# One attention and gating kernel: layer 1's lanes of two samples kept apart, and the output product moved to the head of its place

## Chip, core and metric

The kernel runs on one core of one Trainium2 chip. The metric is the device time of one execution in microseconds (us). Before the change it took 3711.0 us (median of the 3 executions known before the change was run, 3706.7 to 3712.3). Every run told of below was in the fast state, except one that was timed only once and has no state; it is named. Outputs of all kernels were correct.

## The reference, cut to what matters

Four layers are applied to x, four samples of 256 channels of 48 x 48. Each adds its result to x, and each reads x through a group norm.

```python
x = x + L0(gn(x))   # eight-head attention over 2304 places, q and k normalised, then w_out
x = x + L1(gn(x))   # max pool, blur, 81-tap depthwise sums, sigmoid gate, x * gate
x = x + L2(gn(x))   # a second attention, one head
x = x + L3(gn(x))   # depthwise 3 x 3 and norms
```

What matters here: layer 0 is nearly all matmuls; layer 1 has none (for the first three samples), so it can run beside the *next* sample's layer 0 on the other engines. Both write x.

## The kernel before

Layer 0 is cut into groups. A group issues the scores of two key blocks and weighs the values of the two blocks before. Nine groups are a unit (384 queries of two heads), six units a phase (one sample, one pair of heads). Each engine executes its instructions in the order in which the program records them, and the recorder below decides that order.

```python
for t, (u, g, st) in enumerate(groups):
    for j in range(g * G, (g + 1) * G):
        scores(u, j)                     # TensorE, then exp on ScalarE
    if prev is not None:
        add_up(*prev)                    # sums of exps: VectorE, some on GpSimd
    do(due, t)
    ...
    if clock["slot"] == AT_AFTER % NG:   # third group: an early layer-1 step
        lanes([lane for lane in st["others"] if lane[1] == FREE], st, t, ends)
    do(fills, t)                         # the place's products
    lanes(st["others"], st, t + 0.5, ends)   # layer-1 steps
    ... weigh(pu, j) ...
```

The third group of a unit is "the place": it also holds a projection chunk for the next pair of heads and the output product of an earlier unit, sorted by rank.

```python
# chunk: q, then v, then k, squares and the next fetch
return [(1, lambda: qk(s, 0)), (2, lambda: values(s)), (3, end)]

def part(k):                 # one half of the output product
    ps = pj_tile()           # one of two PSUM buffers, in turn
    nc.tensor.matmul(ps[:, :SL], lhsT=wo[...], rhs=o["o"], start=True, stop=True)
    nc.vector.scalar_tensor_tensor(xs, ps[:, :SL], pair["bo"][...], xs, ALU.add, ALU.add)

return [((2.5, 4)[k], lambda k=k: part(k)) for k in range(NK)]
```

Layer 1 of a sample is a generator (a "lane") that takes one step in some groups. Its long middle part is rounds of four products on ScalarE and one sum on VectorE. Rounds may stand in groups with the indices 2, 5, 8 of a unit, for sample 2 in 2, 4, 6, 8; all other steps in `(2, 2, 3, 5, 6, 8)`. With three rounds a unit, a lane does not end within its sample's four phases, and its tail runs beside the next lane.

```python
TURNS, ROUND, HASTE = (2, 2, 3, 5, 6, 8), -1, -2
ROUND_TURNS = {ROUND: (2, 5, 8), HASTE: (2, 4, 6, 8)}
...
if b > 0:
    end = n - 2 if (b, p) == (B - 1, NPAIR - 1) else n + 1
    others.append((l1[b - 1], FREE, 2 if p == 0 else 0, end))
if b > 1 and p == 0:
    others.append((l1[b - 2], FREE, 0, 4 * NG))     # the tail of the lane before
```

Of the kernel before, what the change touches and what calls it, by code (L numbers as in the profile page):

```python
# [17 lines left out]
NK = 2  # L18
# [56 lines left out]
def usual_path(  # L75
# [156 lines left out]
    def scores(u, j):  # L232
        ps = sc_tile()
        for c in range(2):
            for h in range(2):
                r = slice(h * D, (h + 1) * D)
                j0 = j * P + c * D
                nc.tensor.matmul(  # L238
                    ps[c * D : (c + 1) * D, h, :SL], lhsT=u["of"]["k"][r, j0 : j0 + D],
                    rhs=u["of"]["q"][r, u["qc"]],  # L240
                    start=True, stop=True,
                )
        pt = ppool.tile([P, 2, SL], F32, tag="pt", name="pt")
        nc.scalar.activation(pt, ps[:, :, :SL], AF.Exp, scale=u["scale"])  # L244
        u["pt"][j] = pt
# [139 lines left out]
    def attend(phases):  # L385


        groups = []
        for units, work, others in phases:
            for slot, fns in work.items():  # L390
                fills.setdefault(len(groups) + slot, []).extend(fns)
            st = {"others": [[gen, n, a, z, 0, 0] for gen, n, a, z in others], "at": 0}
            groups += [(u, g, st) for u in units for g in range(NG)]
        prev = None

        def lanes(some, st, t, ends):
            for lane in some:
                gen, n, a, z, done, ready = lane
                until = -(-n * (st["at"] + 1 - a) // (z - a))
                clock["final"] = final = st["at"] == z - 1  # L400
                while final or (done < until and t >= ready and not ends):
                    wait = next(gen, None)
                    if wait is None:
                        break
                    done, ready = done + 1, t + wait
                lane[4:] = done, ready

        def do(table, t):

            jobs = [job if isinstance(job, tuple) else (5, job) for job in table.pop(t, ())]  # L410
            for _, fn in sorted(jobs, key=lambda job: job[0]):
                fn()

        for t, (u, g, st) in enumerate(groups):
            for j in range(g * G, (g + 1) * G):
                scores(u, j)
            if prev is not None:
                add_up(*prev)
            do(due, t)

            ends = prev is not None and prev[1] == NG - 1
            clock["t"], clock["slot"] = t, st["at"] % NG

            clock["early"] = True
            if clock["slot"] == AT_AFTER % NG:
                lanes([lane for lane in st["others"] if lane[1] == FREE], st, t, ends)
            do(fills, t)
            clock["early"] = False
            lanes(st["others"], st, t + 0.5, ends)
            st["at"] += 1  # L430
            if prev is not None:
                pu, pg = prev
                for j in range(pg * G, (pg + 1) * G):
                    weigh(pu, j)
                if pg == NG - 1:
                    last(pu, t)
            prev = (u, g)
        pu, pg = prev
        add_up(pu, pg)
        for j in range(pg * G, (pg + 1) * G):  # L440
            weigh(pu, j)
        last(pu, len(groups))
        for t in sorted(set(due) | set(fills)):
            do(fills, t)
            do(due, t)
# [132 lines left out]
    def out_proj(b, p, c, pair, o):  # L578

        cols = slice(c * SL, (c + 1) * SL)  # L580

        def part(k):
            ps = pj_tile()
            nc.tensor.matmul(  # L584
                ps[:, :SL], lhsT=wo[:, p, k * P : (k + 1) * P], rhs=o["o"], start=True,
                stop=True,
            )
            xs = X[b][:, k, cols]
            nc.vector.scalar_tensor_tensor(  # L589
                xs, ps[:, :SL], pair["bo"][:, k : k + 1], xs, ALU.add, ALU.add  # L590
            )

        return [((2.5, 4)[k], lambda k=k: part(k)) for k in range(NK)]

    def l0_unit(b, p, c, pair):
        hold = {}
# [68 lines left out]
    ]  # L665
    L1_BUF = (NT + 1) * AS * AS

    TURNS, ROUND, HASTE = (2, 2, 3, 5, 6, 8), -1, -2
    ROUND_TURNS = {ROUND: (2, 5, 8), HASTE: (2, 4, 6, 8)}

    def paced(gen):

        at, count, wait, turns = -9, 0, 0, TURNS
        while True:
            t, slot = clock["t"], clock["slot"]
            count = count if t == at else 0
            most = turns.count(slot)
            if clock["early"]:
                most = 1 if turns == TURNS else 0
            if not clock["final"] and (t < at + wait or count >= most):  # L680
                yield 0.5
                continue
            wait = next(gen, None)
            if wait is None:
                return
            at, count = t, count + 1
            turns = ROUND_TURNS.get(wait, TURNS)
            yield 0

    def maxima(b, k, res):  # L690
# [60 lines left out]

    def strips(b, k, norm, res):


        haste = HASTE if b == NX - 1 else ROUND
        pd = padded(k, norm, res)

        bufs = [
            lp.tile([P, L1_BUF], F32, tag=tag, name="prod").rearrange("p (n s) -> p n s", s=NT + 1)
            for tag in ("t1", "t2", "t3")  # L760
        ]

        def products(n):
            for i, t in enumerate(ROUNDS[n]):
                dr, dc = TAPS[t]
                nc.scalar.activation(  # L766
                    bufs[n % 3][:, :, min(n, 1) + i].rearrange("p (r c) -> p r c", c=AS),
                    pd[:, PAD + dr : PAD + dr + AS, PAD + dc : PAD + dc + AS],
                    AF.Identity, scale=wt[:, k, t : t + 1],
                )  # L770

        products(0)
        yield haste
        products(1)
        yield haste
        for n, taps in enumerate(ROUNDS):
            last = n == len(ROUNDS) - 1
            if n + 2 < len(ROUNDS):
                products(n + 2)
            to = bufs[(n + 1) % 3][:, :, 0]  # L780
            if last:
                res["acc"] = lp.tile([P, AS, AS], F32, tag="l1acc", name="l1acc")
                to = res["acc"].rearrange("p r c -> p (r c)")
            nc.vector.tensor_reduce(  # L784
                to, bufs[n % 3][:, :, : min(n, 1) + len(taps)], AX.X, ALU.add
            )
            yield haste

    TAPS_AT_ONCE = 12

# [370 lines left out]
    for i, (b, p) in enumerate(order):  # L1161
        work, others = {}, []
        if i + 1 < len(order):
            new = projs[i + 1]
            work[0] = [new["start"]]
            for s in range(NCH):
                work[NG * s + AT_CHUNK] = new["chunk"](s)
            work[NG + AT_CHUNK].append(new["out_bias"])
            for slot, fn in zip((n - 5, n - 3, n - 2, n - 1), new["scale"]):
                work[slot] = [fn]  # L1170
            if i + 2 < len(order):
                work[n // 2] = [projs[i + 2]["prefetch"]]
                work[NG * (NCH - 1) + AT_CHUNK].append(projs[i + 2]["norms"])
        else:
            start, slices = project2(0, norms2[0], twos[0])
            work[1] = [start]
            for s in range(NSL):
                work[NG * s + AT_CHUNK] = slices[s]
        if (b, p) == (2, 0):
            for s in range(NSL):  # L1180
                work.setdefault(s + 2 * NG, []).append(lambda s=s: send(s))
                work.setdefault(s + 5 * NG, []).append(lambda s=s: receive(s))
        if (b, p) == (0, 0):
            others.append((tap_weights(), WEIGHT_TICKS, 2, n - 2))
        if b > 0:
            end = n - 2 if (b, p) == (B - 1, NPAIR - 1) else n + 1
            others.append((l1[b - 1], FREE, 2 if p == 0 else 0, end))
        if b > 1 and p == 0:
            others.append((l1[b - 2], FREE, 0, 4 * NG))
        if (b, p) == (B - 1, NPAIR - 1):  # L1190
            others.append((part(ahead, L1_AHEAD, False), L1_AHEAD, n - L1_AHEAD - 3, n))
        if p == 1 and b + 1 < B:
            others.append((gn(b + 1, norms0[b + 1]), GN_TICKS, 0, n - 2))
        phases.append(([l0_unit(b, p, c, pairs[b][p]) for c in range(NCH)], work, others))
# [1261 lines left out]
```

## Time and profile before

The prediction below shows the profile's lines; this table has what the argument uses. "Wait in places" is worked out from the starts of the score matmuls in the trace: the length of each third group less the length of a free one, that is, of one of the same kind in which TensorE waits for no other engine's late work. A phase with two lanes is called a double phase.

| | before |
|---|---|
| span of the profiled execution | 3710.8 us |
| TensorE busy | 95% |
| phase without layer 1 | 179.0 us |
| phase with one lane | 180 to 184.5 us |
| phases with two lanes | 197.7 and 195.7 us |
| ordinary group, free place | 2.58 us, 8.34 us |
| wait in places, all layer 0 | 40.6 us, 28.2 of it in the two double phases |

TensorE has no slack in layer 0. So each microsecond that it waits in a place is a microsecond of the span, and work that stays on the other engines costs nothing unless TensorE waits for it.

### The profile page before, as it was taken

The numbers are of one execution on the slowest core, as the hardware profiler recorded it, in microseconds if no ns is written. First come the engines' busy times: TensorE is split into PE (matmuls) and PEld (weight loads), VectorE is DVE, ScalarE is ACT, GpSimd is POOL, SyncE is SP. The second block draws the span as 40 slices with busy tenths as digits, with TensorE's granted clock in tenths as the row PEclk, the third lists the DMA queues.
The fourth block names the chain that finished last, engine by engine and source line by source line (L and its number), as shares of the span: only waits on it lengthen the run. The fifth ranks groups of instructions, "written<-read, shape, count | busy, mean of one in ns | idle before, by whom it ended". The sixth has DMA issues, their size and how long they took to land.

```text
span 3710.8 us, 86538 instructions
## 1 busy us (share of the span) xinstructions
PE 3522.4 (95%) x36330; PEld 1759.4 (47%) x36330; DVE 2588.3 (70%) x3203; ACT 2344.5 (63%) x3819; POOL 1444.7 (39%) x900
## 2 busy tenths in 40 slices
PE   7999999999999999999999999999999998999685
PEld 4444444454444444444444444444444445654343
DVE  2455555476778777967787779767968786576687
ACT  4665666666776677557766775587578555555353
POOL 2333333333334333433343334433433455664242
PEclk9999999999999999999999999999999999999797
DMA  4111111111111111121111111111111100000001
GB/s 138 24 25 21 26 21 26 21 25 21 25 21 26 20 29 17 34 55 34 21 25 21 25 21 25 21 25 21 25 16 25 17 6 6 6 8 4 26 29 74
DMA packets 114591, 97.89 MB, mean 26 GB/s; under 512 B 56224, under 2 KB 111632, under 8 KB 112400
## 3 DMA queue, kind: packets, MB, share of 16 engines
q1 hardware_dynamic: 111728, 91.27, 12.8%
q8 instruction: 286, 4.69, 0.5%
q10 hardware_dynamic: 2464, 1.00, 0.1%
q14 instruction: 113, 0.93, 0.1%
HBM read 59.33 MB, written 11.80 MB: 19 GB/s over the span
## 4 chain that ended last, share of the span: by engine, by line
PE 68%; DVE 18%; issue 5%; ACT 4%; POOL 3%; DMA 2%; SPq 0%; DVEq 0%; ACTq 0%; POOLq 0%
PE av L258 26%; PE sc L238 26%; DVE acc L284 7%; PE pj L512 6%; PE pj L584 3%; PE pj L533 3%; DVE sc L1446 2%; PE pj L291 1%; POOL half L269 1%; ACT pt L244 1%; DVE av L1446 1%; DVE acc L278 1%; PE pj L828 1%; ACT prod L766 1%; DMA xs<-in_x_dram 1%
## 5 line engine op out<-in xcount | busy, mean ns | idle before, releaser
L244 ACT ACTIVATE pt<-sc 128x768 f32<-128x768 f32 x1944 | 1476.5, 812 | 814.1 <-PE sc L238 805.4
L269 POOL TENSOR_TENSOR half<-pt 128x768 f32<-128x768 f32 x477 | 954.1, 2001 | 1673.4 <-ACT pt L244 1611.7
L238 PE MATMUL sc<-q,k 64*64 64x384 f32 x13824 | 1279.6, 485 | 12.7 <-ACT pt L244 9.9
L258 PE MATMUL av<-pt,v 64*64 64x384 f32 x13824 | 1279.8, 485 | 0.0
L284 DVE TENSOR_TENSOR acc<-acc,pt 128x768 f32<-128x768 f32 x792 | 930.7, 1175 | 86.2 <-DVE acc L284 1.8
L238 PEld LDWEIGHTS sc<-q,k 64*64 64x64 f32 x13824 | 510.6, 133 | 638.2 <-issue 499.9
L258 PEld LDWEIGHTS av<-pt,v 64*64 64x64 f32 x13824 | 514.4, 133 | 594.0 <-issue 557.3
L284 DVE TENSOR_TENSOR acc<-acc,half 128x768 f32<-128x768 f32 x459 | 468.6, 1021 | 335.7 <-POOL half L269 334.1
L589 DVE SCALAR_TENSOR_TENSOR x<-pj,bo,x 128x384 f32<-128x384 f32 x192 | 118.0, 615 | 461.9 <-PE pj L584 461.7
L512 PE MATMUL pj<-xs,w 128*128 128x384 f32 (+1 forms) x768 | 298.5, 512 | 3.2 <-issue 1.7
L766 ACT ACTIVATE prod<-pd,wt 128x256 f32<-128x256 f32 x486 | 280.6, 743 | 0.2
L339 POOL TENSOR_TENSOR o<-o,rinv 128x384 f32<-128x384 f32 x95 | 128.9, 1356 | 284.3 <-DMA rinv<-rinv 273.2
L512 PEld LDWEIGHTS pj<-xs,w 128*128 128x128 f32 x768 | 131.0, 190 | 157.3 <-issue 53.9
L584 PE MATMUL pj<-o,wo 128*128 128x384 f32 x384 | 159.8, 501 | 33.3 <-DVE x L589 28.7
L258 PE MATMUL av<-pt,qv 64*64 64x384 f32 x1728 | 173.9, 496 | 0.0
L238 PE MATMUL sc<-qv,kd 64*64 64x384 f32 x1728 | 169.4, 486 | 2.4 <-ACT pt L244 2.4
L784 DVE TENSOR_REDUCE prod<-prod 128x256 f32<-128x1280 f32 x114 | 168.5, 1478 | 0.0
L278 DVE TENSOR_TENSOR acc<-pt 128x768 f32<-128x768 f32 x99 | 139.3, 1407 | 26.4 <-ACT pt L244 26.4
L533 PEld LDWEIGHTS pj<-w,xs 128*128 128x128 f32 x1152 | 143.8, 192 | 26.0 <-issue 0.6
L533 PE MATMUL pj<-w,xs 128*128 128x128 f32 x1152 | 144.1, 275 | 0.0
L518 ACT ACTIVATE k<-pj,bias 128x384 f32<-128x384 f32 x96 | 55.7, 580 | 127.5 <-PE pj L512 127.0
L335 POOL TENSOR_TENSOR o<-raw 128x384 f32<-128x384 f32 x95 | 117.7, 1238 | 0.0
(226 smaller groups left out, 2686.7 us busy)
## 6 DMA issues: line engine op xcount, KB each, us to landing
xs<-in_x_dram SPq DMA_DIRECT2D x96, 384.0 KB
rinv<-rinv SPq DMA_DIRECT2D x208, 94.5 KB
x<-in_x_dram SPq DMA_DIRECT2D x6, 1152.0 KB
out_dram<-x SPq DMA_DIRECT2D x6, 1152.0 KB
l<-row SPq DMA_DIRECT2D x416, 1.5 KB
w<-in_wqkv_dram SPq DMA_DIRECT2D x32, 192.0 KB
rinv<-ls SPq DMA_DIRECT2D x208, 1.5 KB
x_out<-x SPq DMA_DIRECT2D x6, 384.0 KB
```

Source lines behind the costliest of these rows:

```text
L238: nc.tensor.matmul(ps[c * D : (c + 1) * D, h, :SL], lhsT=u["of"]["k"][r, j0 : j0 + D], rhs=u["of"]["q"][r, u["qc"]], start=True, stop=True,)
L244: nc.scalar.activation(pt, ps[:, :, :SL], AF.Exp, scale=u["scale"])
L258: nc.tensor.matmul(u["av"][h * D : (h + 1) * D, half, :SL], lhsT=value(u, j, h)[r], rhs=pt[r, h, :], start=j == 0, stop=j == JB - 1,)
L269: nc.gpsimd.tensor_add(half, pts[0], pts[1])
L278: nc.vector.tensor_add(u["acc"], ready[0], ready[1])
L284: nc.vector.tensor_add(u["acc"], u["acc"], term)
L339: eng.tensor_mul(o, o, u["rinv"])
L512: nc.tensor.matmul(ps[:, :n], lhsT=at["w"][:, k, t, :], rhs=xs[s][:, k, :n], start=k == 0, stop=k == NK - 1,)
L533: nc.tensor.matmul(ps[:, i * P : (i + 1) * P], lhsT=xs[s][:, k, i * P : (i + 1) * P], rhs=at["w"][:, k, 2, :], start=k == 0, stop=k == NK - 1,
L584: nc.tensor.matmul(ps[:, :SL], lhsT=wo[:, p, k * P : (k + 1) * P], rhs=o["o"], start=True, stop=True,)
L766: nc.scalar.activation(bufs[n % 3][:, :, min(n, 1) + i].rearrange("p (r c) -> p r c", c=AS), pd[:, PAD + dr : PAD + dr + AS, PAD + dc : PA ...
L784: nc.vector.tensor_reduce(to, bufs[n % 3][:, :, : min(n, 1) + len(taps)], AX.X, ALU.add)
```

## The change

It has two intents. The lanes of two samples shall never run at once: rounds stand in four of nine groups for every sample, and a lane must end in its own last phase. And the output product shall come first in the place, with its addition to x recorded ahead of the group's sums and of the early layer-1 step, so that nothing stands before it.

```diff
-        def do(table, t):
+        def do(table, t, which=lambda rank: True):
 (the jobs that `which` takes are done, the others stay)
         for t, (u, g, st) in enumerate(groups):
             for j in range(g * G, (g + 1) * G):
                 scores(u, j)
+            do(fills, t, lambda rank: rank < 1)
             if prev is not None:
                 add_up(*prev)
-        return [((2.5, 4)[k], lambda k=k: part(k)) for k in range(NK)]
+        return [((0, 4)[k], lambda k=k: part(k)) for k in range(NK)]
-    TURNS, ROUND, HASTE = (2, 2, 3, 5, 6, 8), -1, -2
-    ROUND_TURNS = {ROUND: (2, 5, 8), HASTE: (2, 4, 6, 8)}
+    TURNS, ROUND, ROUND_TURNS = (2, 2, 3, 5, 6, 8), -1, (2, 4, 6, 8)
-                work.setdefault(s + 2 * NG, []).append(lambda s=s: send(s))
-                work.setdefault(s + 5 * NG, []).append(lambda s=s: receive(s))
+                work.setdefault(s, []).append(lambda s=s: send(s))
+                work.setdefault(s + NG, []).append(lambda s=s: receive(s))
-            end = n - 2 if (b, p) == (B - 1, NPAIR - 1) else n + 1
+            end = n - 2 if p == NPAIR - 1 else n + 1
-        if b > 1 and p == 0:
-            others.append((l1[b - 2], FREE, 0, 4 * NG))
```

(Cut: the renaming of `haste` in the rounds, and the body of `do`.)

More of the change, by code (lines that the diff above doesn't have):

```diff
@@ L406, in lanes @@
                 lane[4:] = done, ready
-        def do(table, t):
+        def do(table, t, which=lambda rank: True):
             jobs = [job if isinstance(job, tuple) else (5, job) for job in table.pop(t, ())]
-            for _, fn in sorted(jobs, key=lambda job: job[0]):
+            table[t] = [job for job in jobs if not which(job[0])]
+            for _, fn in sorted((job for job in jobs if which(job[0])), key=lambda job: job[0]):
                 fn()
@@ L686, in paced @@
             at, count = t, count + 1
-            turns = ROUND_TURNS.get(wait, TURNS)
+            turns = ROUND_TURNS if wait == ROUND else TURNS
             yield 0
@@ L752, in strips @@
     def strips(b, k, norm, res):
-        haste = HASTE if b == NX - 1 else ROUND
         pd = padded(k, norm, res)
@@ L772, in strips @@
         products(0)
-        yield haste
+        yield ROUND
         products(1)
-        yield haste
+        yield ROUND
         for n, taps in enumerate(ROUNDS):
@@ L786, in strips @@
             )
-            yield haste
+            yield ROUND
     TAPS_AT_ONCE = 12
```

## The prediction

> **What bounds the kernel now.** I read the page's busy shares and its chain first, then busy time in windows that I cut at the attention's own borders, then the list of waits, then the timeline of single places.
>
> ```profile
> PE 3522.4 (95%) x36330; PEld 1759.4 (47%) x36330; DVE 2588.3 (70%) x3203; ACT 2344.5 (63%) x3819; POOL 1444.7 (39%) x900
> ...
> PE 68%; DVE 18%; issue 5%; ACT 4%; POOL 3%; DMA 2%; SPq 0%; DVEq 0%; ACTq 0%; POOLq 0%
> ```
>
> TensorE is busy 95% of the span and holds 68% of the chain; VectorE has 18% of the chain though it is busy only 70%: it matters in places, not on average. Layer 0 is 16 phases (sample, head pair) of 54 groups, nine groups to a unit. A group (scores and weighing of two key blocks) takes 2.58 us, and the third group of each unit, "the place", takes 8.34 us, as it also holds a projection chunk and the output product of an earlier unit. Cut at phase borders (from the starts of every 16th score matmul):
>
> ```profile
> 586.60:765.60 179.00, 178.95 (x1932) 89.07 (x1928) 91.16 (x124) 108.41 (x172) 58.51 (x38) 1.00 0.14 24
> 765.60:948.70 183.10, 180.78 (x1936) 88.73 (x1932) 132.03 (x173) 115.54 (x187) 70.79 (x40) 1.00 0.13 21
> 948.70:1131.70 183.00, 182.72 (x1936) 86.78 (x1932) 141.15 (x161) 141.48 (x240) 66.30 (x39) 1.00 0.14 23
> ...
> 1498.10:1695.80 197.70, 185.46 (x1944) 89.48 (x1940) 153.54 (x200) 116.13 (x188) 77.59 (x44) 0.97 0.20 44
> ...
> 2245.60:2441.30 195.70, 184.01 (x1944) 89.03 (x1940) 154.78 (x203) 118.22 (x192) 77.29 (x44) 0.98 0.13 22
> ```
>
> Columns: window, length, then busy time of TensorE, weight loads, VectorE, ScalarE, GpSimd, clock, DMA. The first row is a phase without layer 1: TensorE is busy 178.95 of 179.00 us, so that is a floor. Phases with one layer-1 lane take 183 us or so (ten phases, 180 to 184.5). The two rows of 197.7 and 195.7 us are the first phases of samples 2 and 3, in which the old lane's tail and the new lane run together. Here the clock also fell to 0.97 and 0.98.
>
> ```profile
> PEld pj L512 <- ACT v L538: 47.1, 88, 0.5
> ...
> PEld pj L584 <- DVE x L589: 39.4, 18, 7.2
> ...
> PE pj L584 <- DVE x L589: 28.7, 16, 6.6
> ```
>
> These waits (total, times, longest) are what the change is about: the output product's second half (L584) waits until VectorE has added the first half to x (L589), because both use the same one of two PSUM buffers.
>
> **What the Trainium skill says.** "TensorE: Matmul & The Clock Gate", section "Architectural detail", says that VectorE works its queue in strict order; the trace agrees: L589, which needs only a finished product, starts after 2.22 us of layer-1 work (L702) in the timeline below. "SBUF — State Buffer", section "Who interferes with whom", says that a VectorE instruction with two SBUF inputs contends with a GpSimd one that reads SBUF. That agrees with L278, an addition of one fixed shape, which takes 0.95 us in some units and 2.56 us in others, the latter under a GpSimd addition (L269, 1229.39 to 1231.91). "TensorE: Matmul & The Clock Gate", section "Why this matters for your kernels", warns of idle gaps over about 3 us; the trace agrees: the unit from 1527.5 to 1567.2 us, with the 6.6 us wait, has a clock of 0.91, units with waits under 2 us have 1.00. "Perfetto Trace Analysis", section "Matmuls", wants groups to rotate through PSUM banks so that eviction overlaps; here two buffers rotate, and the order decides which eviction is exposed.
>
> **The change part by part.**
> *(a) Two lanes never at once.* Each sample's lane must now end in its own last phase; the order of VectorE's instructions in the changed program shows it finishing in the last unit. The phases at 1498 and 2245 us should then look like the one at 765 us: 197.7 - 183.1 = 14.6 us and 195.7 - 183.1 = 12.6 us, together 27 us, off the path that sets the end. The tail's work (gate, statistics) isn't removed; it moves into the lane's last phase, and may cost there.
>
> *(b) Rounds in four of nine groups (2, 4, 6, 8) instead of three (2, 5, 8)* for the first two samples; the third has it already. Slot by slot, three rounds per unit lengthen the other groups by 0.57 us, four by 0.67 us. About 20 rounds per half: 20/3 x 0.57 = 3.8 against 5 x 0.67 = 3.3 us. Two samples of two halves: 2 us saved. Groups 2, 4, 6, 8 are also those without VectorE's sums, so VectorE is less behind at a phase's first place: the trace's third sample has it (lag about -0.3 us at its second phase, against 3.5 to 4.1 us elsewhere).
>
> *(c) Output product at the head.* This is the place of a free unit, then VectorE in a lagging one:
>
> ```profile
> 591.78 1.47 PE L238 MATMUL sc<-q,k 64*64 64x384 f32 x16
> 593.18 1.56 PE L512 MATMUL pj<-xs,w 128*128 128x385 f32 x4
> 594.59 1.50 PE L533 MATMUL pj<-w,xs 128*128 128x128 f32 x12
> 595.92 0.81 PE L584 MATMUL pj<-o,wo 128*128 128x384 f32 x2
> 596.65 1.56 PE L512 MATMUL pj<-xs,w 128*128 128x385 f32 x4
> 598.05 0.81 PE L584 MATMUL pj<-o,wo 128*128 128x384 f32 x2
> ```
> ```profile
> 1230.17 2.56 DVE L278 TENSOR_TENSOR acc<-pt 128x768 f32<-128x768 f32 x1
> 1232.65 2.22 DVE L702 TENSOR_TENSOR t<-x 128x1222 f32<-128x1222 f32 x1
> 1234.80 0.17 DVE L703 COPY t<-x 128x26 f32<-128x26 f32 x1
> 1234.89 0.60 DVE L589 SCALAR_TENSOR_TENSOR x<-pj,bo,x 128x384 f32<-128x384 f32 x1
> 1236.50 0.62 DVE L589 SCALAR_TENSOR_TENSOR x<-pj,bo,x 128x384 f32<-128x384 f32 x1 [1.01 <-PE pj L584]
> ```
>
> Before: q, v, product 1, k, product 2 (buffers X Y X Y X); product 2 waits for L589. After: product 1, q, v, k, product 2 (X Y X Y X): now v waits for L589, and k and product 2 wait for ScalarE only (the changed program's semaphores say so).
>
> Gain: in the free place k starts 0.73 us after product 1, where the two matmuls' own rate is 2 x 0.32 us, and its first weight load isn't hidden (0.43 against 0.32 us to the next matmul): 0.19 us, by the wait L512 on L538. In the new order each eviction has a full product (1.3 us or more) in between. Some 72 of 96 places without another stall x 0.19 = 14 us.
>
> Cost: measured from the head (end of the scores), L589 can start at 0.85 us, v would start at 0.73 + 1.41 = 2.14, and a waiting matmul starts 0.66 us after L589's start. So VectorE must be free by 1.48 us. Before, the limit was 2.84 (product 1) + 1.47 = 4.3 us, but with that group's own layer-1 step ahead of L589. The sums of the third group are GpSimd's alone, so "ahead of the sums" skips only that step; L278 stays ahead. L278's end after the head, in units of before with the same VectorE work, minus 1.48, is the new stall. Per sample: third unit 3.23 (1.8), fifth 3.62 (2.1), after the first half's gate 3.3 + 0.3 (2.1), next unit about 3 (1.5), the two maxima units 4.06 and 4.60 (2.6 and 3.1), after the second gate 3.27 (1.8): 15 us, over three samples 45 us. Third groups of before lose 40.6 us in all over their floor: 28 us of it in the two double phases, 12.5 us in the others.
>
> *Sum:* -40.6 (all old stalls of the places) + 45 (new ones) - 14 (free places) - 2 (rounds) - 1 (other groups of the double phases) = -12.6 us, about 3698 us. (a) brings its 27 us; (c) gives back half of it: better order in free places, earlier deadline in lagging ones.
>
> **The rivals.**
> First: (c) helps everywhere, as its author meant. For it: the two waits on L589 total 68.1 us; the step it overtakes is up to 2.4 us long. Against: VectorE's lag comes mostly from L278 and the sums before it. If the lag were half as long, new stalls would be near 15 us and the time near 3670.
> Second: the head comes too early for the product's own input. GpSimd's division (L339) waits for the DMA of the reciprocals. In most units it ends 0.3 to 5 us before the head, in seven after it by at most 0.9 us; most of these are lagging units, so it hides beneath the stall. Should it be late by 1 us in a third of the places, that is 30 us: 3730.
> Third: new stalls of 3 us trip the clock, as in the double phases: one slow window of about 3.4 us is 1.7 us, in six places 10 us: 3708.
> Fourth: the copies of sample 0 out and sample 3 in move ahead by two to four units and hold up the reciprocals' DMA. Against: the mean DMA share of that phase is 0.20. Worth 2 us at most.
>
> **Range and chances.** The surest term is (a)'s 27 us; (c) is the difference of 45 us (25 to 60) and 14 us (0 to 18). That gives 3674 to 3722 us for 8 in 10. 2% is 74 us either way, which no combination above reaches: 2% faster, 96% within, 2% slower.
>
> **What would show it.** Right: phases 8 and 12 near 183 us with the clock at 1.00; free places near 8.15 us instead of 8.34; the wait of L512 on ScalarE's v gone; L533 waiting for the addition to x in about seven units per sample, 1.5 to 3 us each. Wrong: no such new wait (then faster than 3680), or the first product waiting for GpSimd's division in many units (then slower than 3720), or a tail that drains at once in a lane's last unit.

## The result, and the profile after

The changed kernel took 3720.9 us (median of 4, 3719.1 to 3722.2), the kernel before 3710.3 us (median of 4). The ratio is 1.0029 with a 95% interval of 1.0012 to 1.0047: slower, by little but clear of the noise. Ratios here and below are those of the record; they go with the means of the fast runs of the same rounds (in the experiments without the profiled run), so they are not quite the ratios of the medians. The line numbers in the changed kernel are three or so higher (L592 is L589, L587 is L584, L536 is L533, L515 is L512).

The phases again, of the changed kernel (window, length, busy time of TensorE, weight loads, VectorE, ScalarE, GpSimd, clock, DMA share, GB/s):

```profile
586.40:764.20 177.80, 177.75 (x1932) 89.52 (x1928) 93.23 (x123) 108.42 (x172) 57.99 (x38) 1.00 0.14 24
764.20:949.50 185.30, 180.35 (x1940) 88.80 (x1936) 132.00 (x177) 119.62 (x195) 69.46 (x40) 1.00 0.14 23
949.50:1140.90 191.40, 183.69 (x1936) 88.56 (x1932) 145.42 (x172) 138.18 (x233) 71.17 (x43) 0.99 0.13 23
...
1511.40:1698.20 186.80, 182.00 (x1940) 90.05 (x1936) 132.03 (x177) 119.65 (x195) 67.87 (x40) 0.99 0.22 48
...
1888.50:2079.60 191.10, 183.97 (x1934) 89.73 (x1930) 139.50 (x168) 135.54 (x227) 63.97 (x39) 0.98 0.13 22
...
2261.20:2446.00 184.80, 180.26 (x1936) 88.73 (x1932) 132.96 (x177) 119.58 (x195) 68.76 (x40) 1.00 0.14 23
```

The double phases are gone (197.7 to 186.8 us, 195.7 to 184.8 us), and a phase without layer 1 is 1.2 us shorter. But other phases with one lane grew from 183 or 184 us to 191 us. The waits (total, times, longest) say for what:

```profile
PEld pj L536 <- DVE x L592: 58.1, 24, 5.9
...
PE pj L536 <- DVE x L592: 44.3, 21, 5.2
```

The first line is of the weight load, the second of the matmul behind it; they are the same stretches of time, so they are not to be added. The wait of the second product on L589 is replaced by one of v (L536) on the same addition. A free place in the new order looks like this:

```profile
591.51 1.47 PE L238 MATMUL sc<-q,k 64*64 64x384 f32 x16
592.91 0.91 PE L587 MATMUL pj<-o,wo 128*128 128x384 f32 x2
593.66 1.46 PE L515 MATMUL pj<-xs,w 128*128 128x385 f32 x4
594.96 1.50 PE L536 MATMUL pj<-w,xs 128*128 128x128 f32 x12
596.29 1.46 PE L515 MATMUL pj<-xs,w 128*128 128x385 f32 x4
597.60 0.81 PE L587 MATMUL pj<-o,wo 128*128 128x384 f32 x2
```

From the first product to the last it takes 0.19 us less than before; all free places are 8.15 us instead of 8.34. The dearest place is the one at 1109.3 us. Its scores end at 1110.6 us, and VectorE is here:

```profile
1107.89 1.75 DVE L892 TENSOR_TENSOR x<-x,l1acc 128x768 f32<-128x768 f32 x1
1109.56 2.56 DVE L284 TENSOR_TENSOR acc<-acc,half 128x768 f32<-128x768 f32 x1
1112.23 3.83 DVE L284 TENSOR_TENSOR acc<-acc,pt 128x768 f32<-128x768 f32 x2
1115.99 0.94 DVE L278 TENSOR_TENSOR acc<-pt 128x768 f32<-128x768 f32 x1
...
1117.12 0.61 DVE L592 SCALAR_TENSOR_TENSOR x<-pj,bo,x 128x384 f32<-128x384 f32 x1
```

A layer-1 step of the ninth group (L892) and then the last sums of the unit before are still to be done. The addition L592 has been moved ahead of the *third* group's step, but these stand before it in either order. TensorE has done the product and q by 1112.9 us and waits. The time from the end of the scores until VectorE has done what is recorded ahead of the addition is called its lag below; here it is 6.3 us (L278 ends at 1116.9).

The 8.1 us between the two profiled spans can be laid out (us):

| part | before | after | difference |
|---|---|---|---|
| waits in places | 40.6 | 62.8 | +22.2 |
| free length of 88 places, 0.19 us each | | | -16.7 |
| other groups, phases with layer 1 | | | +1.7 |
| first phase's other groups, start of the first scores (51.9 to 53.6) | | | +2.7 |
| one place with layer 2's start; all after layer 0 | | | -1.9 |

The last two rows cannot be told from differences between executions: over the traces of all twelve kernels the first scores start at 51.9 to 53.7 us, and what follows layer 0 takes 715 to 723 us.

### The profile page after: what moved, and what is told of

Its sections match the earlier page's. It is cut to its first block, busy times and chain, and to the rows that moved or that the text cites. A ratio compares the mean times of both kernels' runs of the same rounds, so it can differ in the third digit from the quotient of the medians.

```text
span 3718.9 us, 86480 instructions
## 1 busy us (share of the span) xinstructions
PE 3515.1 (95%) x36330; PEld 1770.3 (48%) x36330; DVE 2514.5 (68%) x3203; ACT 2346.0 (63%) x3819; POOL 1426.2 (38%) x900
## 4 chain that ended last, share of the span: by engine, by line
PE 65%; DVE 17%; issue 8%; ACT 5%; POOL 3%; DMA 1%; SPq 0%; DVEq 0%; POOLq 0%; ACTq 0%
PE sc L238 25%; PE av L258 24%; DVE acc L284 6%; PE pj L515 5%; PE pj L536 3%; PE pj L587 3%; POOL half L269 2%; ACT pt L244 2%; DVE sc L1444 2%; ACT prod L766 1%; PE pj L291 1%; DVE av L1444 1%; DVE acc L278 1%; PE pj L828 1%; DMA rinv<-rinv 1%
## 5 line engine op out<-in xcount | busy, mean ns | idle before, releaser
L269 POOL TENSOR_TENSOR half<-pt 128x768 f32<-128x768 f32 x477 | 938.7, 1969 | 1764.3 <-ACT pt L244 1667.7
L284 DVE TENSOR_TENSOR acc<-acc,pt 128x768 f32<-128x768 f32 x792 | 886.5, 1119 | 84.5 <-DVE acc L284 2.3
L592 DVE SCALAR_TENSOR_TENSOR x<-pj,bo,x 128x384 f32<-128x384 f32 x192 | 118.3, 616 | 547.1 <-PE pj L587 547.1
L515 PE MATMUL pj<-xs,w 128*128 128x384 f32 (+1 forms) x768 | 285.3, 496 | 1.7 <-issue 1.7
L536 PE MATMUL pj<-w,xs 128*128 128x128 f32 x1152 | 153.6, 285 | 44.3 <-DVE x L592 44.3
L536 PEld LDWEIGHTS pj<-w,xs 128*128 128x128 f32 x1152 | 148.6, 199 | 77.8 <-DVE x L592 58.1
L515 PEld LDWEIGHTS pj<-xs,w 128*128 128x128 f32 x768 | 141.5, 195 | 80.7 <-issue 6.1
L587 PE MATMUL pj<-o,wo 128*128 128x384 f32 x384 | 166.4, 515 | 4.3 <-ACT qv L955 2.8
L278 DVE TENSOR_TENSOR acc<-pt 128x768 f32<-128x768 f32 x99 | 129.6, 1309 | 11.2 <-ACT pt L244 11.2
L541 ACT COPY v<-pj 128x384 f32<-128x384 f32 x96 | 45.9, 478 | 125.1 <-PE pj L536 125.1
```

Source lines behind the costliest of these rows:

```text
L269: nc.gpsimd.tensor_add(half, pts[0], pts[1])
L278: nc.vector.tensor_add(u["acc"], ready[0], ready[1])
L284: nc.vector.tensor_add(u["acc"], u["acc"], term)
L515: nc.tensor.matmul(ps[:, :n], lhsT=at["w"][:, k, t, :], rhs=xs[s][:, k, :n], start=k == 0, stop=k == NK - 1,)
L536: nc.tensor.matmul(ps[:, i * P : (i + 1) * P], lhsT=xs[s][:, k, i * P : (i + 1) * P], rhs=at["w"][:, k, 2, :], start=k == 0, stop=k == NK - 1,
L587: nc.tensor.matmul(ps[:, :SL], lhsT=wo[:, p, k * P : (k + 1) * P], rhs=o["o"], start=True, stop=True,)
```

## The experiments

Three theories were set against each other. D, the deadline: the position of the product among TensorE's products sets by when VectorE must be free, and at the head that is too early. L, the lanes: packing a lane into its own phases is what lost. V: VectorE's lag binds somewhere whatever the order.

### Parts alone

`lanes_only` takes the head away from the changed kernel:

```diff
-            do(fills, t, lambda rank: rank < 1)
-        return [((0, 4)[k], lambda k=k: part(k)) for k in range(NK)]
+        return [((2.5, 4)[k], lambda k=k: part(k)) for k in range(NK)]
```

> The changed kernel with the output product back in its old place (after q and v), so that only the lanes and the rounds are changed. Theory D (the deadline: a product at the head gives VectorE only 1.5 us to be free, and that is what lost the time): the old order's waits come back at about 5.5 us per sample, 16.5 us in all instead of 40.6 us, the other groups cost 2 us more: 3688 us (3682 to 3695). Rival L (the lanes' new distribution lost the time, as it packs more VectorE steps into one sample's phases, and the head is good): 3715 us or more.

Measured: 3696.1 us, ratio to before 0.9951 (0.9934 to 0.9968). Waits in places come to 20.6 us. Double phases are 183.7 us each, as this view of `lanes_only` has it:

```profile
1506.70:1690.40 183.70, 181.17 (x1937) 88.34 (x1932) 132.65 (x177) 119.67 (x195) 68.51 (x40) 1.00 0.22 49
2244.50:2428.20 183.70, 181.18 (x1936) 88.26 (x1932) 135.42 (x177) 119.61 (x195) 70.26 (x40) 1.00 0.13 22
```

The lanes are a gain, if 8 us less of one than expected; L falls. About half of the miss is waits (20.6 us instead of 16.5), and one place stands out: the sixth unit of the second phase waits 3.8 and 4.9 us for samples 0 and 1 (after their first gate).

`head_only` gives the kernel before the head alone: the changed `do`, its early call, and ranks 0 and 4.

> The kernel before with the output product at the head and nothing else. Theory D: the lags of VectorE behind the head, read from the trace of before, less 1.48 us, add up to 81 us of waits (more by the factor 1.4 by which such waits were under-read for the changed kernel), 40.6 us of old ones go, free places save 17 us: 3733 to 3765 us. Rival L: faster than before, about 3695 us.

Measured: 3759.7 us, ratio 1.0135 (1.0116 to 1.0155). Waits in places are 99.9 us, 47.0 of them in the two double phases. So the head alone costs 47 us by the medians (50 by the ratio), on lanes kept apart 25 us (3720.9 less 3696.1, from two sets of rounds; 29 by the ratios). Most of the difference is in the double phases, which have the longest lags: there the head adds 18.8 us of waits (28.2 to 47.0), on lanes kept apart 6.5 us (2.4 to 8.9).

`head_behind_step` keeps TensorE's new order but not VectorE's:

```diff
             for j in range(g * G, (g + 1) * G):
                 scores(u, j)
-            do(fills, t, lambda rank: rank < 1)
             if prev is not None:
                 add_up(*prev)
```

> The changed kernel with TensorE's new order (output product first) but the addition to x left where VectorE's order had it, behind the third group's layer-1 step. Theory D: each lagging place waits 1 to 2.4 us longer, in seven units per sample: about 3745 us (3735 to 3760). If what VectorE does ahead of the addition does not matter: 3721 us.

Measured: 3767.4 us, ratio 1.0145 (1.0128 to 1.0162), above the expected range, in the expected direction. Its places wait 113.3 us. The early addition is worth about 47 us (3767.4 less 3720.9, again two sets of rounds) *given* that the product is at the head; it does not make up for it.

`rounds_only` is the kernel before with one tuple changed, everything else (a second lane allowed, copies late) as it was:

```diff
-    ROUND_TURNS = {ROUND: (2, 5, 8), HASTE: (2, 4, 6, 8)}
+    ROUND_TURNS = {ROUND: (2, 4, 6, 8), HASTE: (2, 4, 6, 8)}
```

> The kernel before with rounds in groups 2, 4, 6, 8 for the first two samples too; lanes may still run on into the next sample, the copies stay where they were. If the double phases come from the slower rounds alone, the lanes end by themselves in their own phases and this equals the lanes alone: 3696 us (3690 to 3701). If the bookkeeping of lanes or the earlier copies did it: 3708 to 3712 us.

Measured: 3693.6 us, ratio 0.9953 (0.9936 to 0.9970), the same as `lanes_only`. The lanes then end in time by themselves: the two double phases are 183.7 and 183.6 us long. So of the change's first half the four rounds are the working part; the new ends of the lanes and the earlier copies change nothing that these runs can tell.

### The deadline moved

`product_after_q` puts the first product behind q, its addition still ahead of the step, so that VectorE has some 1.3 us more:

```diff
-            do(fills, t, lambda rank: rank < 1)
+            do(fills, t, lambda rank: rank < 2)
-        return [((0, 4)[k], lambda k=k: part(k)) for k in range(NK)]
+        return [((1.5, 4)[k], lambda k=k: part(k)) for k in range(NK)]
```

> The changed kernel with the first product behind q instead of ahead of it (order q, product, v, k, product; its addition still ahead of the layer-1 step): VectorE has until 2.8 us after the head instead of 1.5. Theory D: with the lags of the changed kernel the waits fall from 63 to about 30 us and the free places lose their 0.19 us: 3704 us (3695 to 3712). If the deadline is not what sets the waits: 3721 us or more.

Measured: 3710.8 us, ratio to before 0.9998 (0.9989 to 1.0007); 10 us under the changed kernel. Waits on VectorE fall, to about 21 us beyond the free places; but free places are 8.44 us, and 8.64 in first units, since v now waits for ScalarE's copy of q with only a product in between. The direction is D's; I had not reckoned with the second part.

`late_products` moves the deadline out of the place. On the lanes of `lanes_only`:

```diff
             def end():
-                qk(s, 1)
+                values(s)
                 squares(s)
...
-            return [(1, lambda: qk(s, 0)), (2, lambda: values(s)), (3, end)]
+            return [(1, lambda: qk(s, 0)), (2, lambda: qk(s, 1)), (3, end)]
-        return [((2.5, 4)[k], lambda k=k: part(k)) for k in range(NK)]
+        return [((3.5, 4)[k], lambda k=k: part(k)) for k in range(NK)]
```

Both products come last, so their buffers are wanted again only by the totals of the next group (or by two short products that follow in two units of a phase).

> Lanes of the changed kernel; in the place the order is q, k, v, then both halves of the output product, so that the two buffers that wait for VectorE's additions are next needed a group later. Theory D: nearly all waits on the addition to x go (16.5 us less than with the lanes alone): 3672 us (3665 to 3680), free places 8.3 us. If VectorE's lag is itself the bound (rival V: the sums come too late for the totals whatever the order), no faster than the lanes alone: 3688 us.

Measured: 3677.6 us, ratio 0.9903 (0.9887 to 0.9920). The product's waits on the addition are gone; what is left in the places is 11.0 us (20.6 with `lanes_only`), nearly all of it in places where a short product follows and waits for its buffer. The largest wait of the place's weight loads is now the one on ScalarE's copy of v, 88 times at most 0.5 us, which was as large before the change. In `late_products`:

```profile
PEld pj L586 <- ACT v L540: 47.1, 88, 0.5
PEld pj L474 <- DVE x L591: 12.3, 14, 3.3
PEld pj L497 <- DVE x L591: 10.5, 14, 1.8
```

The last two are the short products. V falls: VectorE does the same work in a shorter span, and TensorE waits less for it. D's direction holds, but the time came out right in part by luck: D counted on 16.5 us less waits and got 9.6. Another 4.2 us come from 28 places with a short product, whose free length fell from 8.97 to 8.82 us, and 2.8 us lie after layer 0, where executions differ by as much.

`late_products_two_lanes` puts that order into the kernel before, two lanes at once and three rounds:

> The kernel before (rounds in three groups, two lanes at once) with the order q, k, v, product, product. Theory D: two lanes hurt only through the buffer that waits for VectorE; with the deadline about 7.6 us after the head, only the lag of 9 to 12 us in the second unit of the double phases still costs, some 6 us each: 3685 us (3678 to 3693). Rival L: two lanes cost 24 us whatever the order: 3700 us.

(Its edit is the diff above, with the lanes and rounds of before.) Measured: 3688.8 us, ratio 0.9932 (0.9915 to 0.9948). The second unit of each double phase still waits 8.8 us; other double-phase places wait nothing. So two lanes cost 11 us more than one at this deadline, against the 17 to 19 us that the rounds saved at the old one (by the ratio and by the medians of `rounds_only`).

`late_and_short_ones_later` also moves the two short groups of products two groups on:

```diff
-            work[NG + AT_CHUNK].append(new["out_bias"])
+            work.setdefault(NG + 4, []).append(new["out_bias"])
-                work[NG * (NCH - 1) + AT_CHUNK].append(projs[i + 2]["norms"])
+                work[NG * (NCH - 1) + 4].append(projs[i + 2]["norms"])
```

> The late products with the two short groups of products that follow them in two places of a phase (bias of the output, bias of v; each needs a buffer that waits for VectorE) moved two groups on. If what is left of the waits there is those two (2.6 and 4.5 us in the sixth units of the second phases, 1.3 us or so in three second units, 1.6 us in the group behind), some 13 us go: 3664 us (3657 to 3671). If the totals two groups later wait for the same additions instead: 3675 us or more.

Measured: 3675.0 us, ratio 0.9901 (0.9884 to 0.9917): a miss, no different from `late_products` as far as these runs tell. The waits did go: places are 8.34 us nearly everywhere, the longest 10.54. But where the short products now stand they lengthen a group by 0.70 us, where in the place they had cost 0.48 us, and there are 29 of them.

### What makes the lag

`no_step_in_9th` keeps layer-1 steps other than rounds out of a unit's ninth group:

```diff
-    TURNS, ROUND, ROUND_TURNS = (2, 2, 3, 5, 6, 8), -1, (2, 4, 6, 8)
+    TURNS, ROUND, ROUND_TURNS = (2, 2, 3, 5, 6, 6), -1, (2, 4, 6, 8)
```

> The changed kernel with the layer-1 step of the ninth group of a unit (the last but two ahead of the place) moved to the seventh. If VectorE's lag at the head is made by the step just ahead of the last sums, the waits of 63 us fall to about 30 us: 3690 us (3683 to 3700). If the lag is made by the sums themselves, slowed by GpSimd: unchanged, 3717 us or more.

Measured: 3711.2 us, ratio to before 0.9998 (0.9989 to 1.0007). A miss: waits fall only from 62.8 to 52.4 us. Places that had lagged are free (the one of 15.5 us is 8.8 us), but others now lag by 4.1 to 4.9 us, after a longer burst in the seventh group. The step next to the last sums is not the cause alone; a burst two groups earlier is not worked off in time either.

`gate_on_vector` takes GpSimd's multiplications (L890) away from beside VectorE's sums, at the price of 0.95 us each on VectorE:

```diff
-                eng = nc.gpsimd if b < NX else nc.vector
+                eng = nc.vector
```

> The changed kernel with the gate's product for the first three samples on VectorE instead of GpSimd: VectorE gets 3 us more work per half, GpSimd's 1.6 to 2.3 us multiplications beside the last sums go. If it is GpSimd's multiplications beside VectorE's sums that stretch the lag to 6.3 us in the unit after the first gate, that unit's lag falls to 4.5 us or less and its place from 15.5 to 12 us or less. If the amount of VectorE's work makes the lag, it rises above 6.3 us.

Looked at once, 3706.0 us (state unknown, no interval; the time isn't used). The trace is: the lag in that unit fell from 6.3 to 3.8 us and its place from 15.5 to 11.4 us, with one more instruction before the head. `gate_on_vector`, the same stretch as above:

```profile
1104.18 0.94 DVE L890 TENSOR_TENSOR x<-x,gate 128x768 f32<-128x768 f32 x1
1105.05 0.95 DVE L892 TENSOR_TENSOR x<-x,l1acc 128x768 f32<-128x768 f32 x1
1105.92 0.94 DVE L284 TENSOR_TENSOR acc<-acc,half 128x768 f32<-128x768 f32 x1
1106.97 4.14 DVE L284 TENSOR_TENSOR acc<-acc,pt 128x768 f32<-128x768 f32 x2
1111.03 0.95 DVE L278 TENSOR_TENSOR acc<-pt 128x768 f32<-128x768 f32 x1
```

L892 went from 1.75 to 0.95 us and the addition of `half` from 2.56 to 0.94 us. More VectorE work, less lag: in this unit 2.5 of the 6.3 us of lag came from additions drawn out beside GpSimd. (The two sums of 4.14 us still overlap with GpSimd's own halves.)

## Why the prediction was right or wrong

The time lay in the stated range, at its upper end, but the sign was wrong: -12.6 us was summed, about +10 us measured. The step that failed is the cost in lagging places, by which the head should have given back half of (a)'s gain: 45 us were reckoned and 62.8 us measured. Against the sum, the waits are 17.8 us more, the free places 2.7 us better, and the other groups of the phases with layer 1 4.7 us worse (1.7 us more instead of 3 less); with the 0.8 us of the last two rows of the table above this makes -12.6 into 8.0 us, as the profiled spans have it. By its steps:

*(a) The double phases.* Right: 197.7 to 186.8 and 195.7 to 184.8 us in the changed kernel, to 183.7 us each with the head undone, where 183 was written. But 26 us off the double phases were worth only 16 to 18 us in all with the head undone (`lanes_only`): part of the work and its waits moved into the lanes' other phases, whose places waited 18.2 us instead of 12.4. The prediction had named this cost and not counted it.

*(b) Four rounds instead of three, 2 us saved.* Not seen: the groups outside the places cost 1.7 us more in the phases with layer 1 (2.8 us more in `rounds_only`, which has this step alone). That a later lag disappears in first units was right in part (1.33 and 1.64 us of waits are left in two of them). What the step missed is that (b) brings (a): `rounds_only` is the whole gain.

*(c) The gain in free places.* Right: 8.34 to 8.15 us, 0.19 us as worked out, in all 88 places (16.7 us) rather than in 72 (14 us). So the 179.0 us of a phase without layer 1, read as a floor because TensorE was busy all through, was none: it is 177.8 us now.

*(c) The cost in lagging places: 45 us.* This is the term that failed; it measured 62.8 us. Its law did not fail. Where the clock stayed at 1.00, the wait of a place is VectorE's lag less 1.48 us to a few hundredths: lags of 3.23, 3.60, 4.14 and 4.33 us waited 1.76, 2.13, 2.68 and 2.87 us. Three things were missing from the sum:

- The clock, named as the third rival and not put into the sum. Seven places waited 1.4 to 1.7 us more than the law. Two places with equal lag show it. Windows of the changed kernel (length, busy times, clock):

```profile
890.50:900.80 10.30, 8.43 (x64) 4.60 (x60) 8.36 (x12) 4.27 (x9) 4.05 (x2) 1.00 0.00 0
1109.30:1124.80 15.50, 10.59 (x64) 6.53 (x60) 10.78 (x13) 5.03 (x11) 5.95 (x3) 0.89 0.00 1
1637.50:1649.40 11.90, 10.04 (x60) 5.89 (x56) 8.28 (x11) 4.27 (x9) 4.08 (x2) 0.86 0.01 1
```

  The first and third have lags of 3.60 and 3.59 us and the same idle time of 1.9 us on TensorE; one takes 10.3 us at a clock of 1.00, the other 11.9 us at 0.86, with 8.4 and 10.0 us of TensorE busy for the same matmuls. Seven times about 1.6 us is 11 us.

  Finer windows of the same trace show what divides them. Between 100 and 2800 us, so in nearly all of layer 0, seven stretches of 3.41 us have a clock of 0.50 and all the rest has 1.00. These are windows laid out in steps of 3.41 us from such stretches:

```profile
1639.94:1643.35 3.41, 1.55 (x7) 0.76 (x6) 3.41 (x4) 0.62 (x2) 1.64 (x1) 1.00 0.00 0
1643.35:1646.76 3.41, 3.41 (x15) 2.80 (x14) 1.38 (x3) 0.48 (x1) 0.00 (x0) 0.50 0.00 0
1209.86:1213.27 3.41, 2.03 (x6) 0.88 (x6) 3.41 (x2) 1.47 (x3) 3.23 (x2) 1.00 0.00 0
1213.27:1216.69 3.42, 2.20 (x15) 1.93 (x16) 1.17 (x2) 0.48 (x1) 0.00 (x0) 1.00 0.00 0
```

  The wait of 1.9 us that cost clock lay wholly in one stretch (1.86 us idle), and the next stretch had half the clock. A longer wait, of 2.6 us from 1211.9 us on, was cut by a border into 1.38 and 1.22 us and cost none (the stretch after these two has 1.00 as well); the first of the three places above had 1.76 us in one stretch and the rest in the next. Between 100 and 2800 us of this trace each of the seven follows a stretch with 1.86 us or more of idle TensorE, and no other stretch had more than 1.76 us. So a wait's length alone does not say whether it costs clock: it is partly luck how it falls. (The ends of matmuls are modelled, so the line between 1.76 and 1.86 us is not a sharp one. In the traces of all twelve kernels, over the same 2700 us, each of 52 stretches with more than 1.92 us idle is followed by a halved one; between 1.65 and 1.92 us 10 of 25 are.)
- The lag after the first gate. The prediction took 3.6 us from units of before that seemed alike; it was 6.3 and 6.7 us for two samples (for the third 3.0 us), 6 us of waits beyond the reckoned ones. `gate_on_vector` shows for the first two that GpSimd beside the sums made it.
- Places not on the list: the statistics of the next sample's norm behind a round in a ninth group (2.0 us, twice) and the two first units above: 7 us. Against that, the "next unit" with 1.5 us per sample waited nothing (-4.5 us); the rest of the terms differ by less.

*The rivals.* "The head helps everywhere" is refuted by `head_only`. "The head comes too early for GpSimd's division" was 0.7 us, once, in the first of the two maxima units: as small as the margins said. The clock was real, and the trace of before had warned of it: the unit from 1567.2 to 1602.1 us, with a wait of 2.0 us, has a clock of 0.95, which the prediction passed over. Its 68.1 us of "two waits on L589" are the weight load's and the matmul's wait for the same addition, in the same stretches, so the argument for the first rival counted them twice; the longer of the two is 39.4 us in all. The copies' earlier place cannot be told from nothing (`rounds_only` against `lanes_only`).

*What it should have tried.* The same sum with the product at the end of the place costs one line to write, and would have shown a deadline of 7 us or more against lags of 3 to 7 us. The best version here, both products last on lanes kept apart, takes 3675 to 3678 us (in two versions) and beats both kernels by about 1%.

What stays open: no run moved a wait against the borders of the clock's stretches, so that cause is read from traces alone; and why two of three samples lag so much more after the first gate is read from one trace each.

## What to carry to other kernels

When two buffers rotate, the instruction that waits is the one two places behind, so put a product whose eviction runs on a lagging engine where its second successor comes late, not first: early issue also means an early deadline. An addition moved up in an engine's order overtakes only what is recorded after its new place; read the engine's lag at that moment, not its average share (here 70%). And when a lane spills over into the next, try its pace first: one tuple here brought the 17 us that were all that the change's first half gained.

## What the Trainium skill lacked or had wrong

- "TensorE: Matmul & The Clock Gate", section "Why this matters for your kernels", warns of idle gaps over about 3 us. Here a gap of 1.9 us was followed by a clock of 0.50 for 3.41 us (1.6 us lost), and one of 2.6 us by none: what set them apart was how much idle time fell into one of the clock's stretches of 3.41 us (1.86 us, against 1.38 and 1.22 us). So shorter gaps can cost too, and the length of the gap alone does not tell.
- "SBUF — State Buffer", section "Who interferes with whom", has the rule, and two slowdowns from separate measurements that differ by the order of issue, but no size for fp32 additions in a kernel. Here one and the same addition (128 x 768) took 0.95 us alone and up to 2.56 us beside GpSimd, and removing three GpSimd multiplications cut a lag of 6.3 us to 3.8 us although VectorE had more to do.
- No page that I found gives the price of a weight load that is kept from running ahead by a wait: two fp32 matmuls in a row start 0.43 us apart instead of 0.32, and with the wait's own 0.08 us that is 0.19 us per place, 16.7 us over 88 places.
